# Two-layer graph network on one core: z ahead of the fetched h, the coming x on ScalarE's queue, row sums by ScalarE, and a later first copy

## The chip, the cores and the metric

The kernel runs on one core of a Trainium2 chip. The metric is device time of one execution in microseconds (us); lower is better. The core has a matmul engine (TensorE, PE in the profile), a vector engine (VectorE, DVE), an activation engine (ScalarE, ACT), a general engine (GpSimd, POOL) and SyncE (SP), which here only issues transfers (DMAs). Each engine works through its own list of instructions in order.

## The reference

There are 16 graphs of 1024 nodes with 128 features. `adj` is a symmetric 0/1 matrix per graph.

```python
# layer 0: gated graph network, 4 rounds
h = max(layernorm(x), 0)
for i in range(4):
    m = adj^T @ (h @ weight[i])
    h = gru_cell(m, h, w_ih[i], w_hh[i], b_ih[i], b_hh[i])
x = x + h * nodemask
# layer 1: graph convolution, 4 rounds
h = max(layernorm(x), 0)
for i in range(4):
    h = relu(adj @ (h @ W[i]) + b[i])
    h = gamma[i] * (h - mean) / sqrt(var + eps) + beta[i]   # mean, var over all graphs and nodes
out = x + h
```

with `gru_cell`: r and z are sigmoids of sums of a part from m and a part from h, n = tanh(x_n + r * h_n), and the new h is (1 - z) * n + z * h.

## The kernel before

**Shapes.** A graph's adjacency matrix is held as 8 row tiles of 128x1024. Features are held as 128x1024 tiles (feature by node, or node by feature), worked on in two halves of 512 columns. What is multiplied with the adjacency is split into a high part (rounded) and a low part (the rest), so one product with a graph's adjacency takes 8 row tiles x 2 parts x 2 halves = 32 matmuls of 128x512 (`aggregate_rows`, L524). The products with the GRU's weights are in plain f32 (`products`, L999); the trace shows each of those as two records.

**Layer 0, half steps.** Two streams, `sa` with the even graphs and `sb` with the odd ones, alternate. In a half step one stream, called `two`, does the gates of its round, half by half, and the other, `one`, does its 32 adjacency matmuls. On PE the order is: gates of half 0, gates of half 1, 32 adjacency matmuls. `clock[0]` counts half steps from 3; 64 of them, with the opening ones, fill the first 1152 us. Half step 13 starts at 222.77 us. In this stage the order on all five engines is the program's (`manual_schedule`), so where a line stands in `half_step` is where it stands in its engine's list.

Each of the gate banks in PSUM (`g_r`, `g_z`, `g_hn`, `g_xn`) exists once. Half 1's matmuls into a bank wait until half 0's result was read: `g_r` and `g_z` by ACT's two sigmoids (L1017 into `r`, L1026 into `z`).

**The exchange of h.** The new h of a half is transposed in blocks by DVE (L720), written by SP to memory (`cross_h`, L591), and read back by SP in four pieces (`n_h`, L598). In the next half step ACT copies the high part from the fetched tile (`high`, L925, or L944 where the input comes from `y_in`), and DVE subtracts to get the low part (`low`, L932 or L948). The adjacency matmuls read these. In the old `half_step` the first half runs on ACT as: r, what is due at "beside0", tanh (L1022), high part of half 0, z. The high part of half 1 is ahead of r of half 1.

**What is hung in.** `agenda` holds work that is due in a half step at a named place ("start", "beside0", "beside1", "late", "gap", "mid"). `plan` puts there the tail of a finished graph (sums, `store_xmid`, `norm_factors`, normalised blocks, `store_ymid`) and the preparation of the coming one: `next_load` (L539, a 512 KB load of x into one of four buffers), `next_sums` (DVE statistics of it), `next_factors`, `next_blocks`. POOL also rounds adjacency rows, and issues the 2 MB store of a transposed adjacency matrix (L629).

**Layer 1.** For each graph 8 tiles are loaded and widened by ACT (L1322) and DVE (L1324) and multiplied. `first_split` (L1381, L1382) makes the high and low part of a graph's input to the first convolution. For graph 0 of the later rounds the multiplication uses unnormalised features, and `raw_weights` then corrects with the row sums of its adjacency matrix, `degree`. These come from `row_sums`: 16 matmuls of a tile of ones with the 8 row tiles (L1418) and two copies (L1422). In this layer the order of PE, ACT and DVE is the scheduler's.

Of the kernel before, what the change touches and what calls it, by code (L numbers as in the profile page):

```python
# [8 lines left out]
F32 = mybir.dt.float32  # L9
F32R = mybir.dt.float32r  # L10
# [6 lines left out]
P = 128  # L17
# [324 lines left out]
def exact_path(  # L342
# [39 lines left out]
    def tmp(name):  # L382
        return ps_t.tile([P, HALF], F32, tag="tmp", name=name)

    adjT_d = [dram.tile([NB, P, N], BF16, tag=f"adjT{b}", name=f"adjT_d{b}") for b in range(B)]
    xmid_d = [dram.tile([N, C], F32, tag=f"xmid{b}", name=f"xmid_d{b}") for b in range(B)]
    ymid_d = [dram.tile([P, N], F32, tag=f"ymid{b}", name=f"ymid_d{b}") for b in range(B)]
# [20 lines left out]
    nc.vector.memset(eps_t, EPS)  # L408
    ones = const.tile([P, 1], F32, tag="ones", name="ones")
    nc.vector.memset(ones, 1.0)  # L410
    low = const.tile([P, (B + 2) * NB], F32, tag="low", name="low")
    nc.vector.memset(low, 0.0)

# [119 lines left out]
    with ExitStack() as st:  # L533
# [46 lines left out]
        def glance(b, stage, js):  # L580

            junk = work.tile([P, N], BF16, tag="junk", name=f"junk{b}_{js[0]}", bufs=1)
            for j in js:
                lows = stage[j % 4].bitcast(U16).rearrange("p (n t) -> p n t", t=2)[:, :, 0]
                k = b * NB + j
                nc.scalar.activation(junk, lows, AF.Copy, accum_out=low[:, k : k + 1])

        def exchange_out(t, name, d=None):
            if d is None:
# [180 lines left out]
        class Stream:  # L770
# [35 lines left out]
                norm_blocks(self.xt, self.y, self.norm, ks)  # L806

            def next_load(self):
                self.next_x = load_x(self.b + 2, nc.gpsimd)

            def next_sums(self):
                self.next_norm = norm_stats(self.next_x, f"in{self.b + 2}")
# [12 lines left out]
            def plan(self, n, tail=None):  # L825

                if tail:
                    b, xt, hT, parts = tail
                    end = {}

                    def sums():
                        end["norm"] = tail_sums(b, xt, hT, parts)

                    def blocks(hf):
                        if hf == 0:
                            end["y"] = y_mid(b)
                        norm_blocks(xt, end["y"], end["norm"], range(hf * BH, (hf + 1) * BH))

                    at(n + 2, "gap", sums)
                    at(n + 3, "mid", lambda: store_xmid(b, xt))  # L840
                    at(n + 3, "gap", lambda: norm_factors(end["norm"]))
                    at(n + 4, "beside0", lambda: blocks(0))
                    at(n + 4, "beside1", lambda: blocks(1))
                    at(n + 5, "mid", lambda: store_ymid(b, end["y"]))
                if self.b + 2 < B:
                    at(n + 4, "late", self.next_load)
                    at(n + 6, "start", self.next_sums)
                    at(n + 6, "gap", self.next_factors)
                    at(n + 7, "beside0", lambda: self.next_blocks(0))
                    at(n + 7, "beside1", lambda: self.next_blocks(1))  # L850
                    at(n + 7, "end", self.ins_away)
# [120 lines left out]
            def gate_step(self, hf, between=None):  # L972
                self.products(hf)
                self.reset_gate(hf)
                if between:
                    between()
                self.candidate(hf)
                self.update_gate(hf)
                self.less(hf)
                self.mixed(hf)  # L980

            def products(self, hf):
# [47 lines left out]
            def less(self, hf):  # L1030
# [3 lines left out]
                else:  # L1034
                    nc.vector.tensor_sub(ho, hin, self.r)  # L1035

            def mixed(self, hf):
                ho = self.now[2]
                nc.vector.tensor_mul(ho, ho, self.z)  # L1039
                self.last_dve = nc.vector.tensor_add(ho, ho, self.r)  # L1040
                if hf == NH - 1:
                    self.hT = self.new
                    self.i += 1
# [28 lines left out]
        def first_step(one, two, gated, halfway):  # L1072

            feed.next_step()
            if one is sa:
                feed.jobs = transposes([(s.b, s.rows) for s in (sa, sb)])
            one.split_step()
            feed.some(2)
            two.gate_step(0)
            two.half_away(0)  # L1080
            if feed.full or (clock[0], "mid") in agenda:
                mids(two)
            feed.some(1)
            two.gate_step(1)
            two.half_away(1)
            due("late")
            gated()
            one.agg_step(0)
            halfway()
            feed.some(NB if one is sa else 1)  # L1090
            one.agg_step(1)
            two.finish()
            clock[0] += 1
# [8 lines left out]
        def half_step(one, two, gated=None, halfway=None):  # L1102

            feed.next_step()
            counts = (2, 1, 1)
            if one is sb and one.i == 0:
                feed.jobs = transposes([(s.b, s.rows) for s in (sa, sb)])
                counts = (0, 0, 0)
            elif two is sb and two.i == 0:
                counts = (2, 2, 1)  # L1110
            elif two is sa and two.i == 1 and two.across:
                counts = (3, 1, 1)
            due("ins")
            due("start")
            if one.i > 0:
                one.halves_back()
            else:
                one.hw = hw_tiles(one.b, f"ghw{one.b}_0")
            two.fetch()
            feed.some(counts[0])  # L1120
            two.products(0)
            two.reset_gate(0)
            due("beside0")
            due("looks")
            two.fetch_more()
            two.candidate(0)
            two.less(0)
            one.high(0)
            two.update_gate(0)
            one.low(0)  # L1130
            two.mixed(0)
            two.half_away(0)
            two.first_four()
            if feed.full or (clock[0], "mid") in agenda:
                mids(two)
            one.high(1)
            feed.some(counts[1])
            two.products(1)
            two.reset_gate(1)
            due("beside1")  # L1140
            two.first_glances()
            due("late")
            one.low(1)
            two.candidate(1)
            two.less(1)
            two.update_gate(1)
            two.last_four()
            two.mixed(1)
            two.half_away(1)
            due("outs")  # L1150
            due("gap")
            due("end")
            if gated:
                gated()
            one.agg_step(0)
            if halfway:
                halfway()
            feed.some(counts[2])
            one.agg_step(1)
            two.finish()  # L1160
            clock[0] += 1
# [4 lines left out]
        with tc.manual_schedule(engines=every):  # L1166
# [115 lines left out]

            sa.plan(0)
            sb.plan(1)
            first_step(sa, sb, looks, lambda: ahead(1))
            first_step(sb, sa, lambda: turn_ih(prep, w_g, 2), lambda: ahead(2))
            written[0] = False
# [89 lines left out]
    def first_split(b):  # L1377
        yt = flat(f"y{b}").rearrange("p k c -> p (k c)")
        nc.gpsimd.dma_start(yt, ymid_d[b])
        hw = hw_tiles(b, f"chw{b}_0")  # L1380
        nc.scalar.copy(hw[0], yt)  # L1381
        nc.vector.tensor_sub(hw[1], yt, hw[0].bitcast(F32))  # L1382
        return hw

# [17 lines left out]
    def raw_weights(i, pm, aff, stats):  # L1402
# [6 lines left out]
            nc.vector.scalar_tensor_tensor(mt[:, cols], degree[:, cols], aff[1], mt[:, cols], ALU.mult, ALU.add)  # L1409
            nc.tensor.matmul(pc[hf], w_c[:, i, :], mt[:, cols], start=True, stop=True)  # L1410
        conv_done(0, i, pc, stats)

    def row_sums(rows):

        pd = [tmp(f"pt_deg{hf}") for hf in range(NH)]
        for j in range(NB):
            for hf in range(NH):
                nc.tensor.matmul(  # L1418
                    pd[hf], ones_r, rows[j][:, hf * HALF : (hf + 1) * HALF], start=(j == 0), stop=(j == NB - 1)
                )  # L1420
        for hf in range(NH):
            nc.scalar.copy(degree[:, hf * HALF : (hf + 1) * HALF], pd[hf])  # L1422

    xo = []

# [29 lines left out]
            for n0, n in pieces(k):  # L1455
                nc.gpsimd.dma_start(xo_piece(k, n0, n), by_node(xmid_d[k], n0, n))

    ones_r = work.tile([P, P], F32R, tag="ones_r", name="ones_r", bufs=1)
    nc.vector.tensor_copy(ones_r, ones.to_broadcast([P, P]))
    degree = w_mT.rearrange("p l c -> p (l c)")[:, :N]  # L1460

    stats = small.tile([P, B * NH, 6], F32, tag="bn_st", name="stats0")
# [1 line left out]
    for b in range(B):  # L1464
        rows = load_adjT(b, 0)
        hw_next = first_split(b + 1) if b + 1 < B else None
        pm = banks(b, 0)
        aggregate(pm, hw, rows, 0)
        if waiting:
            last = first_weights(*waiting, stats)  # L1470
            if b == 1:
                with tc.issue_after(last.ins):
                    sb.rest()
        if b == B - 1:
            hw_next = raw_split(1)
        aggregate(pm, hw, rows, 1)
        if b == 0:
            row_sums(rows)
        hw, waiting = hw_next, (b, pm)


# [112 lines left out]
```

## Time and profile before

| what | value |
|---|---|
| median of 3 runs (lowest, highest) | 1773.89 us (1771.36, 1773.9) |
| profiled execution: its own time | 1774.21 us |
| profiled execution: span of the instructions | 1772.3 us |
| busy in the span: PE, DVE, ACT, POOL | 1754.2, 1288.6, 1108.6, 373.0 us |
| mean granted TensorE clock | 0.998 |
| bytes moved by DMA | 400.16 MB, mean 226 GB/s |

The span runs from the first to the last instruction of the program; the profiled execution's own time has 1.9 us around it. Busy times of engines overlap each other. Ends of matmuls are modelled, so a PE that is shown busy can be waiting for some tenths of a microsecond; the distance between the starts of matmuls is the surer measure.

### The profile page before, as it was taken

The numbers are of one execution on the slowest core, as the hardware profiler recorded it, in microseconds if no ns is written. First come the engines' busy times: TensorE is split into PE (matmuls) and PEld (weight loads), VectorE is DVE, ScalarE is ACT, GpSimd is POOL, SyncE is SP. The second block draws the span as 40 slices with busy tenths as digits, with TensorE's granted clock in tenths as the row PEclk, the third lists the DMA queues.
The fourth block names the chain that finished last, engine by engine and source line by source line (L and its number), as shares of the span: only waits on it lengthen the run. The fifth ranks groups of instructions, "written<-read, shape, count | busy, mean of one in ns | idle before, by whom it ended". The sixth has DMA issues, their size and how long they took to land. (4 is left out here: it accounts for less than half of the span.)

```text
span 1772.3 us, 22314 instructions
## 1 busy us (share of the span) xinstructions
PE 1754.2 (99%) x6734; PEld 1194.8 (67%) x6734; DVE 1288.6 (73%) x2310; ACT 1108.6 (63%) x1713; POOL 373.0 (21%) x415
## 2 busy tenths in 40 slices
PE   9999999999999999999999999999999999999997
PEld 6565656565656565656565656577778888888886
DVE  7676867877777887877787786766666666666665
ACT  5356556556556556655755654486777767767765
POOL 4224223332332331422422323010100000000010
PEclk9999999999999999999999999999999999999999
DMA  7558578677677776766866858788866676757667
GB/s 256 144 155 290 141 204 282 169 214 242 209 204 221 227 202 209 253 194 204 270 182 169 309 147 229 281 280 293 292 228 215 226 249 205 251 211 255 232 221 268
DMA packets 363618, 400.16 MB, mean 226 GB/s; under 512 B 158189, under 2 KB 239889, under 8 KB 363489
## 3 DMA queue, kind: packets, MB, share of 16 engines
q1 hardware_dynamic: 342736, 323.59, 58.5%
q0 software_dynamic: 20224, 74.80, 11.8%
q8 instruction: 55, 0.90, 0.2%
q14 instruction: 75, 0.61, 0.1%
q10 hardware_dynamic: 528, 0.26, 0.0%
HBM read 267.47 MB, written 97.52 MB: 206 GB/s over the span
## 5 line engine op out<-in xcount | busy, mean ns | idle before, releaser
L524 PE MATMUL pm<-row,ghw 128*128 128x512 f32 x2048 | 503.5, 403 | 0.1
L524 PEld LDWEIGHTS pm<-row,ghw 128*128 128x128 f32 x2048 | 384.1, 188 | 105.5 <-issue 29.1
L524 PE MATMUL pc_m<-wide,chw 128*128 128x512 f32 x1024 | 245.3, 395 | 0.0
L615 POOL CAST half<-row 128x1024 bf16<-128x1024 f32 x128 | 141.9, 1120 | 397.8 <-DMA adjT<-half 384.6
L524 PEld LDWEIGHTS pc_m<-wide,chw 128*128 128x128 f32 x1024 | 190.5, 188 | 41.8 <-issue 3.8
L961 ACT COPY m<-pm 128x512 f32<-128x512 f32 x128 | 68.7, 588 | 207.4 <-PE pm L524 207.4
L1018 DVE SCALAR_TENSOR_TENSOR r<-g_hn,vecs,r 128x512 f32<-128x512 f32 x128 | 93.6, 731 | 136.9 <-ACT r L1017 75.5
L1022 ACT ACTIVATE r<-r,vecs 128x512 f32<-128x512 f32 x128 | 92.4, 722 | 158.4 <-DVE r L1019 156.4
L524 PE MATMUL pc_g_r<-wide,chw 128*128 128x512 f32 x464 | 187.1, 403 | 0.3 <-ACT chw L501 0.3
L524 PE MATMUL pc_g_z<-wide,chw 128*128 128x512 f32 x464 | 181.2, 391 | 0.0
L577 POOL CAST row<-stage 128x1024 fp32r<-128x1024 f32 x112 | 128.4, 1154 | 203.7 <-DMA stage<-in_adj_dram 169.1
L1324 DVE CAST wide<-block 128x1024 fp32r<-128x1024 bf16 x160 | 110.0, 692 | 75.4 <-PE pc_m L524 44.7
L1324 DVE CAST wide<-packed 128x1024 fp32r<-128x1024 bf16 x160 | 110.3, 692 | 71.9 <-PE pc_g_z L524 54.1
L1322 ACT CAST wide<-packed 128x1024 fp32r<-128x1024 bf16 x96 | 100.6, 1048 | 58.5 <-PE pc_m L524 28.3
L1322 ACT CAST wide<-block 128x1024 fp32r<-128x1024 bf16 x96 | 100.7, 1049 | 53.7 <-PE pc_g_z L524 27.7
L999 PE MATMUL g_r<-m,w_mT 128*128 128x512 f32 x256 | 130.8, 592 | 0.3 <-ACT m L961 0.3
L999 PE MATMUL g_xn<-m,w_mT 128*128 128x512 f32 x256 | 130.8, 593 | 0.0
L999 PE MATMUL g_z<-m,w_mT 128*128 128x512 f32 x256 | 130.8, 592 | 0.0
L1372 DVE BATCH_NORM_STATS2 stats<-feat 128x6 f32<-128x512 f32 x128 | 84.1, 686 | 47.0 <-ACT feat L1371 45.9
L1017 ACT ACTIVATE r<-g_r,brz 128x512 f32<-128x512 f32 x128 | 87.9, 686 | 41.7 <-PE g_r L999 41.2
L1035 DVE TENSOR_TENSOR h<-h,r 128x512 f32<-128x512 f32 x96 | 83.3, 868 | 41.7 <-ACT r L1022 41.7
L1039 DVE TENSOR_TENSOR h<-h,z 128x512 f32<-128x512 f32 x128 | 106.7, 834 | 6.8 <-ACT z L1026 0.2
(186 smaller groups left out, 2817.9 us busy)
## 6 DMA issues: line engine op xcount, KB each, us to landing
block<-adjT_d SPq DMA_DIRECT2D x256, 256.0 KB, 4.8
packed<-adjT_d SPq DMA_DIRECT2D x256, 256.0 KB, 5.5
stage<-in_adj_dram SPq DMA_DIRECT2D x120, 512.0 KB, 5.4
adjT_d<-adjT POOLq DMA_DIRECT2D x16, 2048.0 KB, 8.1
cross_h<-t_h SPq DMA_DIRECT2D x92, 256.0 KB, 2.2
n_h<-cross_h SPq DMA_DIRECT2D x368, 64.0 KB, 2.1
xmid_d<-x POOLq DMA_DIRECT2D x16, 512.0 KB, 6.3
y<-ymid_d POOLq DMA_DIRECT2D x16, 512.0 KB, 5.3
```

The costliest lines, as they stand in the source:

```text
L524: nc.tensor.matmul(pm[hf], hw[s][:, j * P : (j + 1) * P], rows[j][:, hf * HALF : (hf + 1) * HALF], start=(j == 0 and s == 0), stop=(j == N ...
L577: nc.gpsimd.tensor_copy(t, stage[j % 4])
L615: nc.gpsimd.tensor_copy(t, row.bitcast(F32))
L999: nc.tensor.matmul(po, wT[:, i, g * C : (g + 1) * C], rhs, start=start, stop=stop)
L1017: nc.scalar.activation(r, pr, AF.Sigmoid, bias=brz[:, 3 * i : 3 * i + 1])
L1018: nc.vector.scalar_tensor_tensor(r, phn, b_hn(i), r, ALU.add, ALU.mult)
L1022: nc.scalar.activation(self.r, self.r, AF.Tanh, bias=b_in(self.i))
L1035: nc.vector.tensor_sub(ho, hin, self.r)
L1039: nc.vector.tensor_mul(ho, ho, self.z)
L1322: nc.scalar.copy(r, t)
L1324: nc.vector.tensor_copy(r, t)
L1372: nc.vector.bn_stats(stats[:, b * NH + hf, :], dst)
```

## The change

1. In `half_step`, z of half 0 and the product h*z (split out of `mixed` as `scaled`) come ahead of the high part of half 0. The high part of half 1 comes behind r of half 1.
2. The load of a coming x goes from POOL's queue at "late" of half step n+4 to ACT's queue at "beside0" of half step n+5, and its sums from "start" of n+6 to "gap" of n+5.
3. The 16 matmuls with ones are gone. ACT sums each of graph 0's 8 row tiles with an accumulating copy (128x1024), hung into half steps 5 to 8. The 1024 sums go to memory in half step 9 and come back, broadcast to all partitions, during the first convolution.
4. `first_split`'s copy of the high part is issued on ACT behind `sb`'s last copies of m.
5. `gated` work of the opening half steps comes ahead of what is due at "gap".

```diff
+    degree_d = dram.tile([N], F32, tag="degree", name="degree_d")
...
+        def row_sums(rows, js):
+
+            for j in js:
+                junk = work.tile([P, N], BF16, tag="junk", name=f"summed{j}", bufs=1)
+                nc.scalar.activation(junk, rows[j].bitcast(F32), AF.Copy, accum_out=by_row[:, j : j + 1])
...
             def next_load(self):
-                self.next_x = load_x(self.b + 2, nc.gpsimd)
+                self.next_x = load_x(self.b + 2, nc.scalar)
...
-                    at(n + 4, "late", self.next_load)
-                    at(n + 6, "start", self.next_sums)
+                    at(n + 5, "beside0", self.next_load)
+                    at(n + 5, "gap", self.next_sums)
...
+            def scaled(self):
+                ho = self.now[2]
+                nc.vector.tensor_mul(ho, ho, self.z)
+
             def mixed(self, hf):
                 ho = self.now[2]
-                nc.vector.tensor_mul(ho, ho, self.z)
...
             two.candidate(0)
             two.less(0)
+            two.update_gate(0)
+            two.scaled()
             one.high(0)
-            two.update_gate(0)
             one.low(0)
             two.mixed(0)
             two.half_away(0)
             two.first_four()
             if feed.full or (clock[0], "mid") in agenda:
                 mids(two)
-            one.high(1)
             feed.some(counts[1])
             two.products(1)
             two.reset_gate(1)
+            one.high(1)
             due("beside1")
             two.first_glances()
-            due("late")
             one.low(1)
             two.candidate(1)
             two.less(1)
             two.update_gate(1)
             two.last_four()
+            two.scaled()
             two.mixed(1)
             two.half_away(1)
             due("outs")
+            if gated:
+                gated()
             due("gap")
             due("end")
-            if gated:
-                gated()
...
+            for n, place, js in (
+                (5, "beside1", (0,)),
+                (6, "beside0", (1,)),
+                (6, "beside1", (2,)),
+                (6, "gap", (3,)),
+                (7, "gap", (4, 5, 6)),
+                (8, "start", (7,)),
+            ):
+                at(n, place, lambda js=js: row_sums(sa.rows, js))
+            at(9, "mid", lambda: nc.gpsimd.dma_start(degree_d.rearrange("(j p) -> p j", p=P), by_row))
...
-        nc.scalar.copy(hw[0], yt)
+        with tc.issue_after(sb.last_m.ins):
+            nc.scalar.copy(hw[0], yt)
...
-    def row_sums(rows):
-
-        pd = [tmp(f"pt_deg{hf}") for hf in range(NH)]
-        for j in range(NB):
-            for hf in range(NH):
-                nc.tensor.matmul(
-                    pd[hf], ones_r, rows[j][:, hf * HALF : (hf + 1) * HALF], start=(j == 0), stop=(j == NB - 1)
-                )
-        for hf in range(NH):
-            nc.scalar.copy(degree[:, hf * HALF : (hf + 1) * HALF], pd[hf])
...
-    ones_r = work.tile([P, P], F32R, tag="ones_r", name="ones_r", bufs=1)
-    nc.vector.tensor_copy(ones_r, ones.to_broadcast([P, P]))
...
-        if b == 0:
-            row_sums(rows)
+        if b == 2:
+            nc.gpsimd.dma_start(degree, degree_d.partition_broadcast(P))
```

More of the change, by code (lines that the diff above doesn't have):

```diff
@@ L410, in exact_path @@
     nc.vector.memset(ones, 1.0)
+    by_row = const.tile([P, NB], F32, tag="by_row", name="by_row")
     low = const.tile([P, (B + 2) * NB], F32, tag="low", name="low")
@@ L979, in gate_step @@
                 self.less(hf)
+                self.scaled()
                 self.mixed(hf)
@@ L1139, in half_step @@
             two.reset_gate(1)
+            one.high(1)
             due("beside1")
             two.first_glances()
-            due("late")
             one.low(1)
```

## The prediction

> **What bounds the kernel.** I read the page first, then the waits of PE, then the timelines around each wait. The page:
>
> ```profile
> PE 1754.2 (99%) x6734; PEld 1194.8 (67%) x6734; DVE 1288.6 (73%) x2310; ACT 1108.6 (63%) x1713; POOL 373.0 (21%) x415
> PEclk9999999999999999999999999999999999999999
> ```
>
> PE is busy in all but 18.1 of 1772.3 us, at full granted clock. So time can go only in two ways: fewer PE instructions, or fewer waits of PE. An undisturbed half step of layer 0 takes 17.57 us from start to start (half step 7 starts at 117.33, 8 at 134.90, 9 at 152.48). Of the 18.1 us, about 10 lie in the last 28 us, where the output is turned and stored; the change does not touch them. The waits of PE by who ended them:
>
> ```profile
> PE g_z L999 <- ACT z L1026: 3.6, 4, 1.8
> PE pt_wm L486 <- ACT w_both L480: 0.7, 1, 0.7
> PE g_r L999 <- ACT m L961: 0.3, 1, 0.3
> ```
>
> The largest is for z. The timelines of ACT and PE in half step 13 show how it comes about:
>
> ```profile
> 227.43 0.72 ACT L1022 ACTIVATE r<-r,vecs 128x512 f32<-128x512 f32 x1
> 232.09 0.62 ACT L925 CAST ghw<-n_h 128x512 fp32r<-128x512 f32 x1 [3.94 <-DMA n_h<-cross_h]
> 232.62 0.68 ACT L1026 ACTIVATE z<-g_z,brz 128x512 f32<-128x512 f32 x1
> ```
> ```profile
> 230.50 1.02 PE L999 MATMUL g_xn<-m,w_mT 128*128 128x512 f32 x2
> 233.35 1.12 PE L999 MATMUL g_z<-h,w_hhT 128*128 128x512 f32 x2 [1.83 <-ACT z L1026]
> ```
>
> ACT ended tanh at 228.15, then stood 3.94 us before the high part of the fetched h, and z, which needed nothing from it, came behind. PE needed `g_z` at 231.36. The fetch was late because POOL had issued three transfers in a row:
>
> ```profile
> 218.30 0.89 POOL L629 DMA_DIRECT2D adjT_d<-adjT  x1 [2.97 <-DMA adjT<-half]
> 219.18 0.89 POOL L752 DMA_DIRECT2D xmid_d<-x  x1
> 220.06 0.89 POOL L539 DMA_DIRECT2D x<-in_x_dram  x1
> ```
>
> That is 2 MB, 512 KB and 512 KB; the store of h issued by SP at 221.75 landed at 230.90, 9.2 us later, where the median is 2.2.
>
> **The change, part by part.** The sum is made against the profiled execution, 1774.2 us (0.3 above the median of the runs).
>
> *Matmuls with ones:* removed outright from the bounding engine.
>
> ```profile
> L1418 PE MATMUL pt_deg<-wide,ones_r 128*128 128x512 f32 x16 | 3.9, 397 | 0.0
> ```
>
> The first starts at 1163.53 and the next adjacency matmul at 1167.28: 3.75 us. The record before starts at 1163.12 and such records start 0.23 apart, so PE also waited about 0.2 for `ones_r`, which DVE wrote until 1163.33. Minus 3.9 us.
>
> *z ahead:* half steps start late by their length over 17.57: half step 13 takes 222.77 to 242.47, 2.13 more; 21 takes 365.48 to 383.42, 0.37 more; 29 takes 506.43 to 524.96, 0.96 more; and in 5, where opening work is mixed in, the matmul into `g_z` starts 0.71 late. Sum 4.2 us. (The page's 3.6 counts from modelled ends, and 0.6 of it lies in the opening gates at 29.5, where the order stays.) With z right behind tanh it ends at 228.9 in half step 13, 2.5 us before PE needs it. What is late next is the adjacency product: undisturbed it starts 9.91 us into the half step, 232.68 here, and the high part ends at 232.71, the low part 0.7 later, which its third matmul needs at about 233.2. So 0.2 to 0.3 us of the wait stays in half step 13; in 21 and 29 the high part ends at 8.2 and 8.8 us into the half step, and nothing stays. The product h*z, 0.69 us on DVE, now precedes the low part; the smallest room there is 1.4 us in the half steps without a wait. In half 1 the high part moves behind r, and its room before the ninth matmul's row is 3.5 us or more. The low part of half 1 has least, 0.3 us in half step 29, but there DVE also gains the 0.69 us of the product moved ahead and an r that no longer queues behind a late fetch. Minus 4.2, plus 0.2.
>
> *x on ACT's queue:* 14 loads. POOL loses 0.89 us each, which nobody waits for. ACT gains an issue each: its only DMA issue in the trace took 0.43 us, and SP's issues during the jam at 222 to 227 took 1.3 to 1.5. They stand in ACT's list between r and tanh, where ACT idles 1.82 us in an ordinary half step, and in half step 13 is filled by 1.64 us of blocks. There tanh and z move by up to 1.5 us, inside the 2.5 us of room. Cost 0. The sums on DVE keep their place between the last transpose of a half step and the first gate operation of the next; the load is now issued about 15 us ahead of them (225.8, then 241.4), and loads of x landed within 8.0 us (median). The x load leaves the jam (3 MB becomes 2.5 MB at 218 to 228) and comes about 6 us later, between the fetches of h. Bounds: it frees the fetch by the 2.9 us that x landed behind `xmid_d` (228.30 and 231.23), or it costs the fetch the 5.4 us that a 512 KB load of SP's takes to land. I take no change in arrival, because the bytes ahead of the fetch get fewer while others come beside it; worth 0.
>
> At this place a page speaks against the change. The Trainium skill, "DMA: Bandwidth & Descriptors", section "Queues, rings and completion order", says each DMA engine goes round the rings that have work, a packet from each; x on ACT's own ring would then take turns with SP's fetch of h instead of lining up behind the 2 MB store on POOL's ring. By the row above (9.2 us for a small store beside 3 MB) that rings share fairly is not plain. By the rule, waits of the old size would stay and the sum would be about 1770 instead.
>
> *Row sums on ACT:* 8 accumulating copies. The nearest rows are the glances (L586), 1053 ns each for 128x1024 and 188 for reading the accumulator, overlapping so that they follow each other every 1.16 us. They fill idle time of ACT. The tightest place is "gap" of half step 7 with three of them, 3.5 us:
>
> ```profile
> 128.88 1.28 ACT L668 ACT_TABLE_LOAD   x1
> 130.18 0.30 ACT L668 ACTIVATE rs_in<-mv_in,eps_t 128x8 f32<-128x8 f32 x1
> 134.87 1.07 ACT L961 COPY m<-pm 128x512 f32<-128x512 f32 x2 [4.39 <-PE pm L524]
> ```
>
> 4.39 minus 3.5 leaves 0.9 us. The eighth stands between these copies of m and r of half step 8; r, which ended at 137.94, ends at 139.1, and PE writes `g_r` again at 140.06. Behind r, two glances and the blocks of x fill ACT until 150.7, and the next copies of m are due at 152.44. Cost 0; without this cover the eight would cost 9.3 us. The store of the sums in half step 9 is 1024 elements of 4 bytes, unlike any row; I bound it by nothing and by the 2 us that one late fetch cost in half step 13, and take 0, since only one half step is near it. The broadcast back has a graph's time to land.
>
> *Copy behind the last m:* the old copy stood ahead of m in the second last half step.
>
> ```profile
> 1122.24 1.05 ACT L1381 CAST chw<-y 128x1024 fp32r<-128x1024 f32 x1 [6.04 <-PE pm L524]
> 1123.19 1.07 ACT L961 COPY m<-pm 128x512 f32<-128x512 f32 x2
> ```
>
> PE's matmul on m started 0.5 us late at 1123.82, and the next 0.1: minus 0.6. But the copy and its subtraction, 1.21 us on DVE (done at 1124.5, when DVE was idle), now fall at 1142, where DVE works without a gap from 1141 to 1159. `sb`'s last h comes that much later, and the turns of it at 1151.84 and 1155.52, which had 0.4 to 0.7 us of room, would hold PE; the scheduler may put convolution matmuls ahead. Also the widened rows of graph 1 no longer have 3.9 us of ones to catch up behind. Between 0 and 3.9, I take 0.5, as rows are widened in 0.69 us (DVE) and 1.05 (ACT) and used in 0.9.
>
> *Sum:* 1774.2 - 3.9 - 4.2 + 0.2 - 0.6 + 0.5 = 1766.2 us.
>
> **The rivals.** *The wait moves.* If the fetch of h arrives 1 to 2.5 us later in half steps 13, 21, 29 and 5, PE waits at the adjacency product instead, and the 4.2 us come back: 1770.2. For it: the high part has only 2 us of room in those half steps. Against: x leaves the jam. *The turn of the layers gives it back.* Rows of graph 1 or `sb`'s last h arrive late and take the 3.9 us again: 1770 too. For it: DVE is full there. Against: ACT and DVE together widen a row faster than PE uses it. *Slower:* x on its own ring delays the fetched h in every half step that loads, beyond its room. The high part's room before PE is 4.2 us ordinarily, 2 to 3 in the jammed half steps (3 and 4 in each round of 8). Fourteen loads delayed the full 5.4 us lose some 1.2 us each ordinarily and 2.4 to 3.4 in the seven jammed, 7 x 1.2 + 7 x 2.9 = 29 us at worst; it decides for slower once the mean loss passes (8.0 + 3.5)/14 = 0.8 us per load. At 1 us each: 1766.2 + 14 = 1780. Against: 8 us of room in most, and the loads of x at "late" of half step 13 already ran beside exchanges, whose stores landed in 3.1 us instead of 2.2.
>
> **How the numbers follow.** Forecast 0.73, the wait moves 0.12, the turn of the layers 0.09, slower 0.06. About 0.2%, or 3.5 us, is what a measurement of this kernel can tell from no change; the edge is 1770.3. The forecast is faster in all, the next two lie at the edge, half faster and half same or a little over: faster 0.84, same 0.10, slower 0.06. Range: down to 1763.8, if also the 0.7 us for `w_both` goes, the 0.5 at the turn is not lost and a run has 1 us less of chance waits, up to 1771.0, which takes in both middle rivals.
>
> **What would show it.** Right: no row for L1418; PE's waits for z gone but for the opening one; half steps 13, 21, 29 within 0.3 us of 17.57; PE busy lower by 3.7. Wrong: a new wait of PE for the high part or low part (ACT or DVE `ghw`) in half steps 13 and 14 of each 8, for `m` at the end of half step 7, or for `wide` or the turned h between 1140 and 1170 us.

## The result, and the profile after

The changed kernel takes 1775.17 us (median of 17 runs, 1772.92 to 1779.72). The kernel before, run beside it, takes 1771.86 us (17 runs, 1770.22 to 1774.15). The ratio is 1.0018, with a 95% interval from 1.0011 to 1.0024: a little slower, where 1766.2 us and a range up to 1771.0 were forecast. The profiled execution of the kernel after took 1774.15 us with a span of 1772.1; that of before had 1772.3, and was itself 2.3 us above its median.

The page of the kernel after, first the busy times, then the queue that carries most transfers (packets, MB, share of 16 engines' span):

```profile
PE 1751.0 (99%) x6718; PEld 1190.1 (67%) x6718; DVE 1275.3 (72%) x2309; ACT 1120.8 (63%) x1729; POOL 369.0 (21%) x404
q1 hardware_dynamic: 342736, 323.59, 60.9%
```

The 16 matmuls are gone (x6718 for x6734) and PE is busy 3.2 us less, at the same mean granted clock (0.998 in both profiles). The span hardly moved, so PE waits more than before. The line of q1 is the important one, and I had not looked at it before predicting. In the kernel before it reads:

```profile
q1 hardware_dynamic: 342736, 323.59, 58.5%
```

The packets and the bytes are the same. The share times the span is 1036.8 us per DMA engine before (0.585 x 1772.3) and 1079.2 after (0.609 x 1772.1), 4% more time for the same work.

PE's waits of the kernel after, by who ended them (total, times, longest):

```profile
PE g_z L1008 <- ACT z L1035: 3.6, 3, 1.5
PE pm L526 <- DVE ghw L940: 1.2, 2, 0.7
```

The wait for z, which the change was to take away, is as large as before, but elsewhere. Half step 13 now takes 17.57 us, as forecast. Half steps 21 and 37 take 19.33 and 19.36, and 29, 54 and 61 take 18.0 to 18.6. The timelines of ACT, and then of PE, in half step 21:

```profile
364.96 0.69 ACT L1026 ACTIVATE r<-g_r,brz 128x512 f32<-128x512 f32 x1
369.41 0.42 ACTq L541 DMA_DIRECT2D x<-in_x_dram  x1
369.93 1.65 ACT L688 ACTIVATE y_mid<-x,ms_mid,rs_mid 128x128 f32<-128x128 f32 x4 [4.29 <-DMA cross_h<-t_h]
371.49 0.70 ACT L1031 ACTIVATE r<-r,vecs 128x512 f32<-128x512 f32 x1
372.10 0.67 ACT L1035 ACTIVATE z<-g_z,brz 128x512 f32<-128x512 f32 x1
```
```profile
370.34 1.02 PE L1008 MATMUL g_xn<-m,w_mT 128*128 128x512 f32 x2
372.82 1.12 PE L1008 MATMUL g_z<-h,w_hhT 128*128 128x512 f32 x2 [1.46 <-ACT z L1035]
```

z does come right behind tanh, and it no longer waits for the fetched h. But tanh itself is late: r ended at 365.65, and the issue of x came only at 369.41, 0.1 us after a store of h that SP had issued at 364.55 landed (369.31); ahead of the issue ACT waits on the semaphore that this store reports to, and that the load of x reports to as well. The blocks, tanh and z stand behind that issue in ACT's list. A late transfer still decides, through another instruction.

### The profile page after: what moved, and what is told of

It reads as the page before. It is cut to its first block, busy times and chain, and to the rows that moved or that the text cites. A ratio compares the mean times of both kernels' runs of the same rounds, so it can differ in the third digit from the quotient of the medians.

```text
span 1772.1 us, 22284 instructions
## 1 busy us (share of the span) xinstructions
PE 1751.0 (99%) x6718; PEld 1190.1 (67%) x6718; DVE 1275.3 (72%) x2309; ACT 1120.8 (63%) x1729; POOL 369.0 (21%) x404
## 3 DMA queue, kind: packets, MB, share of 16 engines
q1 hardware_dynamic: 342736, 323.59, 60.9%
## 5 line engine op out<-in xcount | busy, mean ns | idle before, releaser
L623 POOL CAST half<-row 128x1024 bf16<-128x1024 f32 x128 | 147.3, 1162 | 413.4 <-DMA adjT<-half 398.6
L1044 DVE TENSOR_TENSOR h<-h,r 128x512 f32<-128x512 f32 x96 | 76.1, 793 | 74.7 <-ACT r L1031 74.6
```

The lines of the kernel that those rows point to most:

```text
L623: nc.gpsimd.tensor_copy(t, row.bitcast(F32))
```

## The experiments

They were run in three sets, each beside the kernel before, whose median was 1773.0 to 1773.4 us there. Ratios are to that median; kernels of different sets are compared by their ratios too.

**The parts, one by one.** I first held two theories. W: the load of x, on ACT's queue and beside the fetches, takes the gain. Its rival R: the loss lies in another part of the change.

*The kernel after without the moved load.*

```diff
-                self.next_x = load_x(self.b + 2, nc.scalar)
+                self.next_x = load_x(self.b + 2, nc.gpsimd)
...
-                    at(n + 5, "beside0", self.next_load)
-                    at(n + 5, "gap", self.next_sums)
+                    at(n + 4, "late", self.next_load)
+                    at(n + 6, "start", self.next_sums)
```

> The changed kernel with the load of x back on POOL's queue at "late" of half step n+4 and its sums back at "start" of n+6; all else stays changed. Theory W (ACT's list stands at the issue of x until a DMA of another engine has landed, and tanh and z stand behind it; x also takes turns with the fetch of h): the waits of PE for z at half steps 21, 29 and 37 and for the low part at 54 go, together 4 to 6 us, so about 1769 to 1770, below the kernel before. Rival R (the load is harmless; the row sums on ACT, the new order or the later copy cost the time): 1775 as in the changed kernel.

It took 1784.96 us, ratio 1.0063 (1.005 to 1.0077): 8 us more than the kernel after by the ratios (1.0063 and 1.0018), 10 by the medians, against W and more than R allowed. The wait is at the high part:

```profile
PE pm L526 <- ACT ghw L933: 9.5, 6, 3.0
```

*The kernel before with the moved load alone* (the same lines, the other way).

> The kernel before with only the load of x moved (ACT's queue, "beside0" of n+5, sums at "gap" of n+5). Theory W: slower than before by 4 to 7 us, about 1776 to 1779, with waits of PE for z in half steps 13, 21, 29, ... longer than before. Rival R: as before within 1 us, 1772.

1773.27 us, ratio 0.9996 (0.9987 to 1.0005). Alone, the load costs nothing, so W fell.

*The kernel before with z ahead alone.*

```diff
-            one.high(0)
             two.update_gate(0)
+            two.scaled()
+            one.high(0)
             one.low(0)
```

> The kernel before with only the order of z, h*z and the high parts changed. Theory W: the waits for z go and nothing replaces them, 1 to 2 us faster than before (the 17 runs of before hold some 2 us less of such waits than its profiled run), 1770. Rival Z (the new order makes the low part late, as the waits for the low part at half steps 54 and 61 suggest): equal or slower, 1772 to 1775, with PE waiting at pm for ghw.

1769.50 us, ratio 0.9979 (0.997 to 0.9988): 3.9 us gained, as the forecast's term for z says. Half steps 5, 13, 21 and 29 are down to 18.74 (opening work included) and three times 17.57 us.

*The kernel before with the row sums alone.*

```diff
+    degree_d = dram.tile([N], F32, tag="degree", name="degree_d")
...
+    by_row = const.tile([P, NB], F32, tag="by_row", name="by_row")
...
+                nc.scalar.activation(junk, rows[j].bitcast(F32), AF.Copy, accum_out=by_row[:, j : j + 1])
...
-        if b == 0:
-            row_sums(rows)
+        if b == 2:
+            nc.gpsimd.dma_start(degree, degree_d.partition_broadcast(P))
```

> The kernel before with only the row sums moved to ACT and the matmuls with ones gone. Theory W: 3.7 us faster than before, 1768. Rival S (the sums on ACT delay m or r, or the output stage gives the gain back, as it took 1.7 us longer in the profile of the changed kernel): 1771 to 1773.

1803.94 us, ratio 1.0179 (1.0165 to 1.0193): 30 us slower, from an edit that removes 16 matmuls. The waits of PE:

```profile
PE g_z L1007 <- ACT z L1034: 21.6, 8, 4.0
```

The sums run in half steps 5 to 9, but half steps 13, 29, 37 and 45 take 23.3 to 24.3 us. Something lasting had changed, and q1's time was up here too (0.604 x 1799.6 = 1087 us). The work on ACT had ended; what lasts is the two new tiles. `degree_d` shifts the tensors behind it in memory by 4 KB. `by_row` is 8 x 4 = 32 bytes per partition, in front of `low`, and shifts every later tile on the chip by 32 bytes: by the addresses in the compiled kernels, `x` starts at byte 35328 before (138 x 256) and at 35360 after; rows, halves, `t_h`, `n_h` and `adjT` likewise go from multiples of 256 to 32 beyond one.

**The shift.** Theory A: transfers to and from such tiles take longer, so each fetch of h comes later. Rivals: D, the shift in memory; S, the sums on ACT.

*The kernel before with nothing but a spare tile.*

```diff
+    spare = const.tile([P, 8], F32, tag="spare", name="spare")
+    nc.vector.memset(spare, 0.0)
     low = const.tile([P, (B + 2) * NB], F32, tag="low", name="low")
```

> The kernel before with one more tile of 32 bytes per partition in front of `low`, set to zero once and never read: all large tiles behind it start 32 bytes further, at 32 instead of 0 modulo 256 bytes. Theory A (the place of the tiles: transfers to and from tiles that start off a multiple of 256 bytes take longer, so the fetch of h comes late): share of queue q1 60 to 61% instead of 58.5, PE waits for z behind a late fetch in half steps 13, 29, 37, 45 of 3 to 7 us each, time 1790 to 1815 us. Rival D (the 4 KB tile `degree_d` in memory moves the other tensors there) and rival S (the accumulating copies on ACT delay something): neither is in this kernel, so 1772 to 1775 us and share 58.5%.

1806.63 us, ratio 1.0185 (1.0168 to 1.0202). A tile that nothing reads costs 33 us. Rows of its page and waits, then ACT and PE in half step 13:

```profile
PE 1761.7 (98%) x6734; PEld 1195.5 (66%) x6734; DVE 1276.4 (71%) x2311; ACT 1108.7 (62%) x1713; POOL 370.4 (21%) x415
q1 hardware_dynamic: 342736, 323.59, 60.2%
```
```profile
PE g_z L1001 <- ACT z L1028: 23.6, 9, 4.5
```
```profile
228.51 0.72 ACT L1024 ACTIVATE r<-r,vecs 128x512 f32<-128x512 f32 x1
234.62 0.62 ACT L927 CAST ghw<-n_h 128x512 fp32r<-128x512 f32 x1 [5.39 <-DMA n_h<-cross_h]
235.15 0.68 ACT L1028 ACTIVATE z<-g_z,brz 128x512 f32<-128x512 f32 x1
```
```profile
235.88 2.08 PE L1001 MATMUL g_z<-h,w_hhT 128*128 128x512 f32 x2 [3.28 <-ACT z L1028]
```

ACT is busy as long as before (1108.7 and 1108.6 us), so ACT does not work slower. The DMA time is up: 0.602 x 1802.0 = 1085 us against 1037. By size of packet (times of q1's packets in the two traces, over 16 engines), 25 of these 47 us lie in the packets of 256 bytes, 19 in those of 512, and 2 in those of 2048 and 4096 together. The transposes of adjacency halves, in 128 issues of 1024 packets of 256 bytes by that count, show it in the time to landing; first the kernel before, then the one with the spare tile:

```profile
adjT<-half SPq DMA_TRANSPOSE x128, 2.8
```
```profile
adjT<-half SPq DMA_TRANSPOSE x128, 3.3
```

A 64 KB piece of h went from 2.1 to 2.3 us. The 2 MB store of a transposed matrix waits for these transposes. It was issued 1.3 to 3.1 us later against half steps 21, 29 and 45, so nearer to their fetch of h, but not against half step 13. ACT's wait for the fetch in half step 13 is 5.39 us where it was 3.94, and that is z's delay in the old order. Half steps 13, 21, 29 and 45 take 22.7 to 23.9 us; the excess of all half steps from 13 on is 30.4 us, against 3.5 in the profile of before.

Not all of that is waiting. Between the two spans (1772.3 and 1802.0) lie 29.7 us: 22.2 of idle PE, 20.0 of them waits for z, and 7.5 in which PE is busy longer on the same 6734 instructions. The two matmuls behind the wait above took 2.08 us, where they took 1.12 before. The granted clock tells why (a window, its length, busy time of PE, PEld, DVE, ACT and POOL, granted clock, share and GB/s of the DMA engines):

```profile
235.70:239.00 3.30, 3.12 (x5) 1.51 (x5) 3.13 (x6) 2.76 (x7) 1.89 (x4) 0.50 0.60 118
```

Four of this kernel's five waits of more than 3 us ran into such a stretch of 3.4 us at a granted clock of 0.50. At half the clock each costs up to 1.7 us, an estimate, so together up to 6.8 of the 7.5.

*The kernel after with `by_row` padded to 256 bytes.*

```diff
-    by_row = const.tile([P, NB], F32, tag="by_row", name="by_row")
+    by_row = const.tile([P, 64], F32, tag="by_row", name="by_row")[:, :NB]
```

> The kernel after with `by_row` padded from 32 to 256 bytes per partition, so that the large tiles start at multiples of 256 bytes as before; `degree_d`, the accumulating copies and x on ACT's queue stay. Theory A: share of q1 near 58%, median landing of a piece of h back at 2.1 us, time 1764 to 1769 us (the forecast of the change as it was made). Rivals D and S, or x on ACT's queue as the cause: as the kernel after, 1774 to 1777 us.

1766.54 us (1765.94 to 1767.44), ratio 0.9963 (0.995 to 0.9976). This is the whole change, and it is faster than both kernels; 1766.2 had been forecast. Page, waits, and ACT in half step 21, to be set against the kernel after:

```profile
PE 1748.5 (99%) x6718; PEld 1191.4 (68%) x6718; DVE 1288.3 (73%) x2309; ACT 1121.2 (64%) x1729; POOL 365.9 (21%) x404
q1 hardware_dynamic: 342736, 323.59, 58.8%
```
```profile
PE g_z L1008 <- ACT z L1035: 0.6, 1, 0.6
```
```profile
364.53 0.69 ACT L1026 ACTIVATE r<-g_r,brz 128x512 f32<-128x512 f32 x1
366.10 0.42 ACTq L541 DMA_DIRECT2D x<-in_x_dram  x1
366.62 1.65 ACT L688 ACTIVATE y_mid<-x,ms_mid,rs_mid 128x128 f32<-128x128 f32 x4 [1.41 <-DVE r L1027]
368.79 0.67 ACT L1035 ACTIVATE z<-g_z,brz 128x512 f32<-128x512 f32 x1
```

The issue of x comes 0.9 us behind r instead of 3.8. z ends at 369.45, 1.3 us before PE needs it, and only the opening wait of 0.6 is left.

*Row sums alone, padded* (that line in the experiment of 1804 us).

> The row sums alone (the experiment at 1804 us) with `by_row` padded to 256 bytes per partition. Theory A: 1773.4 - 3.9 = 1769.5 us, range 1768 to 1771, half steps 13, 29, 37, 45 as in the kernel before. Rivals D and S: 1795 to 1805 us.

1772.47 us (1769.83 to 1776.19), ratio 0.9998 (0.9989 to 1.0007). The padding alone gave 31 us, which leaves D and S at most the 3 us by which this run misses its expectation. The 3.9 us of the matmuls did not show, though: in its profile the turn of the layers is shorter by 3.1, but half steps 12 and 13 lose 1.4 more than before, and 38 and 61 another 1.8. The former led to the store of the sums, below.

*The padded kernel after with the load undone.*

> The kernel after with x back on POOL's queue at "late" (the experiment at 1785 us) and `by_row` padded to 256 bytes per partition. Theory A: z, row sums and first copy without the load, 1764 to 1768 us. Rivals D and S: 1782 to 1788 us. Beside the padded kernel after it shows what x on ACT's queue costs or brings: theory W2 (ACT's issue of x holds tanh and z when it comes late) 1 to 3 us more in the padded kernel after than here; no difference if the landing of x is all that counts.

1767.21 us (1766.37 to 1768.03), ratio 0.9967 (0.9954 to 0.998): as with the moved load, 1766.54. Where tiles lie well, the place of the load makes no difference that can be measured. Under the shift it was worth 8 to 10 us (1784.96 and 1775.17).

*A spare tile of 64 bytes.*

```diff
+    spare = const.tile([P, 16], F32, tag="spare", name="spare")
```

> The kernel before with a spare tile of 64 bytes per partition (the experiment with 32 bytes took 1806.6 us): the large tiles start at 64 modulo 256. If only multiples of 256 bytes are good, as the Trainium skill's page on descriptors would have it: share of q1 about 60% and 1795 to 1815 us. If a multiple of 64 bytes is enough: share 58.5% and 1772 to 1775 us.

1802.40 us, ratio 1.016 (1.014 to 1.0179).

```profile
q1 hardware_dynamic: 342736, 323.59, 60.1%
```

64 bytes off costs nearly as much as 32: q1 takes 1078 us (0.601 x 1794.2). The Trainium skill, "DMA: Bandwidth & Descriptors", section "How a descriptor splits into AXI transactions", says that a transaction must start at a multiple of 256 bytes, so that for a piece that starts elsewhere the first transaction begins at the boundary below and what it fetches ahead of the piece is not used. The direction agrees with this run. The runs show the time, not the transactions, and the time is not one price for every piece: the median packets of 256 and of 2048 bytes took 18 and 84 ns both before and here. 128 bytes was not tried.

**Two further questions.**

*The store of the sums in half step 60* (row sums alone, padded; then the whole change, padded).

```diff
-            at(9, "mid", lambda: nc.gpsimd.dma_start(degree_d.rearrange("(j p) -> p j", p=P), by_row))
+            at(60, "mid", lambda: nc.gpsimd.dma_start(degree_d.rearrange("(j p) -> p j", p=P), by_row))
```

> The row sums alone with `by_row` padded to 256 bytes (the experiment at 1772.5 us), the 4 KB store of the sums in half step 60 instead of 9. Theory: that store, in pieces of 4 bytes, took 14.4 us to land and held the load of adjacency rows and the exchange beside it, so that the transposed matrix of half step 13 left 1.0 us later against the half step and the waits for z grew by 1.5 to 2 us; without it 1769.5 us (1768 to 1771), half steps 12 and 13 as in the kernel before (17.57 and 19.7). Rival: the 3 us lie in chance waits or elsewhere in the row sums; then 1772 to 1773 us.

> The padded kernel after (1766.5 us) with the same store moved to half step 60. With z ahead no half step of it loses time behind that store, so 1765 to 1767 us, no difference that can be measured; if the store costs the padded kernel after the same 3 us, 1763 to 1764 us.

1784.14 us, ratio 1.006 (1.0047 to 1.0073), and 1775.84 us, ratio 1.0018 (1.0009 to 1.0027): both some 10 us worse, where a gain or nothing was expected. POOL, ACT and PE of the second one:

```profile
1065.71 0.90 POOL L637 DMA_DIRECT2D adjT_d<-adjT  x1 [5.20 <-DMA adjT<-half]
1066.60 0.89 POOL L1306 DMA_DIRECT2D degree_d<-by_row  x1
1067.48 0.89 POOL L760 DMA_DIRECT2D xmid_d<-x  x1
```
```profile
1083.59 0.62 ACT L933 CAST ghw<-n_h 128x512 fp32r<-128x512 f32 x1 [11.79 <-DMA n_h<-cross_h]
```
```profile
1084.26 9.52 PE L526 MATMUL pm<-row,ghw 128*128 128x512 f32 x32 [8.10 <-ACT ghw L933]
```

The 4 KB store landed at 1083.08, 16.5 us after its issue, and the piece of h that SP issued at 1067.08 landed at 1083.57. Half step 61 took 27.92 us instead of 17.57. In half step 9 the same store took 13.3 us to land (padded kernel after). Beside it, in the padded row sums alone, four issues of SP took 11 us:

```profile
173.05 11.09 SPq L612 DMA_DIRECT2D h_in<-pair_in  x4
```

In the padded kernel after no half step near it is longer for that. The first of the two kernels had half steps 12 and 13 at 17.57 and 17.90 us (18.03 and 20.66 with the store in half step 9). That fits the supposition, but does not show it: in one profile each, half step 13 took 19.70 us in the kernel before, without any such store, and 17.57 with the load moved alone. The new place was worse, and that is clear. What the row sums bring with no such store was not tried, so the 3 us that the padded row sums miss stay unexplained in part.

*The kernel after (32 bytes) with x issued by POOL at the new place.*

```diff
-                self.next_x = load_x(self.b + 2, nc.scalar)
+                self.next_x = load_x(self.b + 2, nc.gpsimd)
```

> The kernel after (`by_row` of 32 bytes) with x at the same place of the same half step, but issued by POOL. Theory W2: in the kernel after ACT's issue of x waits for transfers that the shift has made late (2 to 3.8 us behind r in half steps 21, 29, 37, 45), tanh and z stand behind it, and PE waits 3.6 us for z; from POOL this goes: no wait for z but the opening one, 1771 to 1773 us. Rival: the landing of x beside the fetch is what costs, whoever issues it: 1774 to 1777 us.

1780.69 us, ratio 1.0046 (1.0034 to 1.0059): worse than from ACT. The wait for z is down to the opening 0.6, as theory W2 had it, but a new one came. DVE and PE around half step 38:

```profile
670.91 0.29 DVE L672 BATCH_NORM_STATS2 st_in<-x 128x6 f32<-128x128 f32 x1 [4.57 <-DMA x<-in_x_dram]
```
```profile
674.88 1.12 PE L1008 MATMUL g_hn<-h,w_hhT 128*128 128x512 f32 x2 [2.06 <-DVE r L1027]
```

POOL stands behind the transposes of adjacency halves, issued x only at 661.70, and the sums at "gap" wait for it on DVE in front of the gates (32.5 us in 11 waits). Sums at "gap" of n+5 need the load on an engine that is free at that time.

## Why the prediction was wrong

**The step that failed** is the row sums: "They fill idle time of ACT ... Cost 0". The engine times were right, and no wait of the kinds named (m at the end of half step 7, r of half step 8) appeared. What the sum has no term for is the tile that holds the result. Its 32 bytes shift every later tile, and q1's transfers take 4 to 5% longer (1079 and 1085 us against 1037). In the kernel before that costs 33 us, since z stands behind a fetch of h that has no room in the jammed half steps, and the granted clock drops behind the longest waits. In the changed order it costs some 9 us (1775.17 against 1766.54 padded is 8.6; the ratios to before, 1.0018 and 0.9963, make it 9.8): it costs the row sums alone 31 us (1803.94 and 1772.47), with z and the copy 17 to 18 (1784.96 and 1767.21), and with the moved load 9 to 10. By profile, the 8.0 us between the two spans are mostly half steps 21 and 37 (1.8 each), 29, 54 and 61 (0.5 to 1.0 each), the opening, and 1.1 us in the output, whose last stores land later.

**The other terms**, read by the padded kernel after against before:

| term | forecast, us | measured, us |
|---|---|---|
| z ahead, half steps 5, 13, 21, 29 | -4.2 + 0.2 | -4.5 |
| first copy behind the last m, half step 64 | -0.6 | -0.6 |
| matmuls with ones and the turn (first convolution matmul to the first one with weights: 15.77, then 12.15) | -3.9 + 0.5 | -3.6 |
| output (28.6, then 29.2 from the first turn of the output to the end) | 0 | +0.6 |
| sum, and difference of the spans (1772.3, 1764.1) | -8.0 | -8.1, -8.2 |

These sizes stand: with the tiles in place the change brings 0.37% (6.5 us), and the shift takes that and 0.18% (3.2 us) more.

**x on ACT's queue**, "no change in arrival", was wrong in part, at no cost where the tiles lie well. Where `sb` loads x, the load runs beside the fetch. In half step 14 the high part starts 6.95 us into the half step in the padded kernel and 6.00 with the load undone, so the load holds it up by 0.95; the rest of the difference to the kernel before (5.06) is the new order, with z ahead. In half steps 30 and 38 it is 0.6 and 0.9 us, while in 22 the high part starts 0.8 earlier. In the kernel after it starts at 8.73; of the 4.24 us of room before, 2.33 are left in the padded kernel and 0.56 in that one. The rule of rings in turn, weighed ahead of the forecast, would make the fetch late there, but these few tenths in single profiles do not settle it; in half step 13 the waits it spoke for did not come back. The issue's wait for earlier transfers (0.9 to 3.8 us behind r) was not foreseen either; "up to 1.5 us, inside the 2.5 us of room" was too little: z moves by 1.2 to 2.0 us in the padded kernel (half steps 13 to 53), which is inside that room, and by up to 4.1 in the kernel after, which is not.

**The store of the sums**, "by nothing and by the 2 us", had an upper end far too low: 10.4 us in half step 61, from the store in half step 60. The forecast value of 0 in half step 9 holds with z ahead; without it one profile suggests some 1.4 us, which chance can make too.

**The rivals.** "The wait moves" came nearest in kind, at z and at the low part, but its cause was not the landing of x. "The turn gives it back" did not happen. The slower rival's victim, the fetched h, cost 1.2 us at the low part in half steps 54 and 61, of which 54 loads x; but where the tiles lie well the same load costs nothing, so x is not the culprit by itself. The three terms named for the lower end of the range add up to 1764.0 us, not 1763.8; nothing hangs on that.

## What to carry to other kernels

A new tile is an edit to every tile placed behind it: before costing a change, look up where the large tiles start, and keep small tiles at the end or padded so that what transfers use starts at a multiple of 256 bytes. When an edit's loss lies in stages that it doesn't touch, compare the queue rows of the two pages first: the same packets and bytes at a larger share is a sign that is easy to miss in the timelines of the engines. Count a long wait of PE at more than its length where the granted clock falls behind it. A transfer of a few KB in pieces of 4 bytes belongs where nothing urgent is in flight.

## What the runs showed of the hardware

- The same 342736 packets and 323.59 MB of q1 took 1026 to 1040 us per DMA engine (share times span) in the eight kernels whose large tiles start at multiples of 256 bytes, and 1078 to 1104 us in the six that are 32 or 64 bytes off. The groups do not overlap. In the kernel with the spare tile of 32 bytes, 44 of the 47 us more lie in packets of 256 and 512 bytes.
- From about the end of waits of PE of 3.3 to 4.5 us the granted clock was 0.50 for 3.4 us, four times in that kernel; its fifth wait over 3 us (3.04) was not followed by such a stretch, and neither were two of 3.35 and 3.74 us with the tile of 64 bytes.
- A store of 4 KB in 4-byte pieces took 11 to 17 us to land, and a 64 KB fetch issued 0.5 us behind it landed 16.5 us later.
- The issue of x on ACT stood 0.9 to 3.8 us behind r in ten half steps (four of the kernel after, six padded), each time until 0.1 us after a store issued by SP had landed. In the trace both report to the same semaphore.
